# A three-layer graph network kernel: exact bf16 parts of the state transposed by DMA instead of TensorE, s spread through DRAM, and four groups under way in a written order of turns

## The chip, the cores and the metric

The kernel runs on one core of a Trainium2 chip. The metric is the device time in microseconds (us) of the program; lower is better. Below, PE is TensorE (PEld its weight loads), DVE is VectorE, ACT is ScalarE, POOL is GpSimd, and SP is SyncE, which issues the DMAs here.

## The reference, cut to what matters

There are 128 graphs of 128 nodes with 256 features each, in float32, and one 128x128 adjacency of zeros and ones per graph. Layer 0 normalizes x, runs three rounds of a gated graph network, and adds the result to x. Layer 1 normalizes again, runs one graph attention with scores from a single number per node, and adds its result.

```python
h = relu(layernorm(x))
for i in range(3):
    m = h @ weight[i]
    aggr = einsum('bst,bsd->btd', A, m)       # A = (adj != 0)
    gi = aggr @ w_ih.T + b_ih;  gh = h @ w_hh.T + b_hh
    r = sigmoid(i_r + h_r);  z = sigmoid(i_z + h_z)
    n = tanh(i_n + r * h_n)
    h = (1 - z) * n + z * h
x = x + h
h = relu(layernorm(x))
Wh = h @ W
s = Wh.sum(-1)
e = where(adj == 0, -inf, leaky_relu(s[:, :, None] + s[:, None, :], 0.2))
x = x + softmax(e) @ Wh
```

## The kernel before

**Tiling.** The graphs are worked on in 32 groups of four (`G = 4`, `NG = 32`). The state of a group lives in two forms: `rows`, with the nodes on the partitions, and `hT`, with the features on the partitions; both are 128 partitions x 1,024 float32. The weights are composed once at the start (`weights`): weight[i] and w_ih become one matrix for each round (`s_x0` to `s_x2`), beside `s_hh` for w_hh.

**A round (layer) of one group** has these steps:

- `node_sums` (L546 to L550) forms sums and differences of blocks of hT (tile `hs`, on POOL) and later of the edge sums (tile `gs`, on DVE).
- `edge_sums` (L498) multiplies by the adjacency. The adjacency is exact in bf16. The state is made so by splitting it into three bf16 parts: the upper halves of its float32 words, read in place with a stride (`top`), the upper halves of what is left (`r1`, POOL, L505), and what is left after that (`p3`, POOL, L508). Three bf16 matmuls then add up to the float32 result (L517, 24 matmuls a round), which ACT copies to `aT` (L521).
- `products` (L593) computes all gates with seven block products instead of eight (`hs` and `gs` are what this needs) in six PSUM banks `x_`, `y_` and `q_`, each for `rz` and `n`; ACT copies banks out (L613) and DVE adds (L616). Its matmuls stand on L576, or on L583 in the last layer, which produces rows.
- `gru` (L650) or, in the last layer, `gru_rows` (L687) applies the gates on ACT and DVE and writes the new hT, or x1.
- `T_to_rows` (L478) turns the new hT back into rows: eight TensorE transposes against an identity (L486) into two PSUM banks, and two ACT copies (L490). The first layer's hT comes from its rows in the same way in `rows_to_T` (L465, transposes on L472, copies on L475).

**The attention** (L764) computes s, one number per node (L772), spreads it across the partitions with four TensorE transposes per group (L781), adds and masks on DVE (L793 to L801), takes the exponential of the whole 128x512 tile on ACT (L803), masks and sums on DVE (L805, L807), transposes the result (L815), and multiplies (L532, L828).

**What sets the order.** Every step is entered in a list with its engine, a planned duration in ns and the buffers that it reads and writes (`op`). A planner (`Plan.run`) then simulates the engines and writes out one fixed order per engine. Gate products form a chain with due times: a turn of one group and one layer has 18,150 ns, and the turn number comes from `phase`. All other steps get a rank from the due times behind them, with a lead of `MARGIN`. Buffers of kind "all" rotate, those of kind "set" rotate by group, "free" ones are given to whoever comes first, and "turn" ones are given in the order of the turns. Three groups are under way (`SETS = 3`); a group's layers stand two turns apart:

```python
late = int(g == NG - 2 and layer > 0) - int(g == NG - 1)
return 3 * g + 2 * layer + late
```

So between two layers of a group there is one turn of another group. All DMAs are issued by SP, in order: x and the adjacency of a group (L737, L739), and the output (L836).

## Time and profile before

| | us |
|---|---|
| median of 3 runs | 2231.08 |
| runs | 2229.99 to 2231.71 |
| profiled execution | 2230.82 |
| its span | 2229.0 |

The mean granted clock of TensorE in the profiled execution is 0.995 of full speed. The costliest groups that bear on the change read as follows on the page (line, engine, operation, output<-input, shapes, count, then busy us, mean ns of one, and the idle time of that engine just before them with its releaser):

```profile
L546 POOL TENSOR_TENSOR hs<-hT 128x512 f32<-128x512 f32 x96 | 133.4, 1390 | 830.8 <-DVE hT L684 802.6
L505 POOL TENSOR_TENSOR r<-rows 128x512 f32<-128x512 f32 x192 | 209.8, 1106 | 38.2 <-ACT rows L490 27.2
L508 POOL TENSOR_TENSOR p<-r 128x512 bf16<-128x512 f32 x192 | 197.9, 1050 | 5.2
L517 PE MATMUL misc<-a,rows 128*128 128x128 bf16 x768 | 136.9, 219 | 0.1
L490 ACT COPY rows<-misc 128x512 f32<-128x512 f32 x128 | 74.4, 584 | 100.5 <-PE misc L486 96.9
```

The 830.8 us before L546 are idle time of POOL, which isn't needed then. A mean on PE is the time of one matmul from start to end, and neighbours overlap. The DMA issues of the page are (output<-input, queue, count, KB each, median us from issue to landing):

```profile
xt<-in_x_dram SPq DMA_DIRECT2D x32, 512.0 KB, 3.8
out_dram<-x SPq DMA_DIRECT2D x31, 512.0 KB, 3.0
at<-in_adj_dram SPq DMA_DIRECT2D x32, 256.0 KB, 2.9
```

### The profile page before, as it was taken

The page shows a single profiled execution, that of the slowest core. Times are in us where ns is not written, and L with a number is a line of the kernel's source. Part 1 is how long each engine was busy: PE and PEld are TensorE (multiplying, and loading weights), DVE is VectorE, ACT ScalarE, POOL GpSimd, SP SyncE. Part 2 cuts the span into 40 slices and gives each one's busy share as a digit, 9 for nine tenths or more (in the row PEclk, how much of TensorE's full clock was granted, in tenths as well). Part 3 has the DMA queues.
Part 4 walks back from the last instruction along what each step waited for, and adds up shares of the span by engine and source line. Part 5 has one row for each costly group of instructions (what it writes and reads, how often), then busy time and mean ns, then how long its engine had stood idle before and what let it go on. Part 6 is the DMA issues. An engine that isn't in the chain of part 4 may idle for free. (4 is left out here: it accounts for less than half of the span.)

```text
span 2229.0 us, 34912 instructions
## 1 busy us (share of the span) xinstructions
PE 2201.2 (99%) x13414; PEld 1967.8 (88%) x13414; DVE 1623.3 (73%) x3330; ACT 1295.0 (58%) x2396; POOL 909.0 (41%) x889
## 2 busy tenths in 40 slices
PE   8999999999999999999999999999999999999996
PEld 6889998889998889998899988899988899988895
DVE  5587777877677877677777778776778776778667
ACT  4565656655656655566656566556566555666454
POOL 5354444343434343434344443434343434344321
PEclk9999999999999999999999999999999999999998
DMA  3000000000000000000000000000000000000000
GB/s 105 10 15 20 25 17 23 15 24 20 24 15 25 15 20 25 25 15 24 15 20 25 20 19 15 25 20 24 15 24 15 20 24 24 15 20 10 11 11 19
DMA packets 55671, 47.59 MB, mean 21 GB/s; under 512 B 3280, under 2 KB 55248, under 8 KB 55504
## 3 DMA queue, kind: packets, MB, share of 16 engines
q1 hardware_dynamic: 55504, 45.36, 6.5%
q8 instruction: 105, 1.72, 0.3%
q14 instruction: 62, 0.51, 0.1%
HBM read 28.58 MB, written 16.78 MB: 20 GB/s over the span
## 5 line engine op out<-in xcount | busy, mean ns | idle before, releaser
L546 POOL TENSOR_TENSOR hs<-hT 128x512 f32<-128x512 f32 x96 | 133.4, 1390 | 830.8 <-DVE hT L684 802.6
L616 DVE TENSOR_TENSOR t_rz<-t_rz,q_rz 128x512 f32<-128x512 f32 x192 | 131.6, 685 | 268.2 <-ACT t_rz L613 229.0
L613 ACT COPY t_rz<-y_rz 128x512 f32<-128x512 f32 x192 | 111.8, 583 | 318.7 <-PE y_rz L576 224.0
L719 POOL TENSOR_TENSOR x<-xt,u 128x512 f32<-128x512 f32 x64 | 84.8, 1324 | 357.6 <-ACT u L715 357.6
L505 POOL TENSOR_TENSOR r<-rows 128x512 f32<-128x512 f32 x192 | 209.8, 1106 | 38.2 <-ACT rows L490 27.2
L508 POOL TENSOR_TENSOR p<-r 128x512 bf16<-128x512 f32 x192 | 197.9, 1050 | 5.2
L576 PE MATMUL y_rz<-hs,s_hh 128*128 128x256 f32 x768 | 199.0, 381 | 0.0
L576 PE MATMUL y_rz<-gs,s_x 128*128 128x256 f32 x768 | 197.2, 379 | 0.0
L576 PEld LDWEIGHTS y_rz<-gs,s_x 128*128 128x128 f32 x768 | 145.7, 190 | 19.7
L576 PEld LDWEIGHTS y_rz<-hs,s_hh 128*128 128x128 f32 x768 | 138.9, 190 | 15.4 <-ACT t_rz L613 0.3
L616 DVE TENSOR_TENSOR t_n<-t_n,q_n 128x512 f32<-128x512 f32 x192 | 131.2, 683 | 13.4 <-ACT t_n L613 7.9
L517 PE MATMUL misc<-a,rows 128*128 128x128 bf16 x768 | 136.9, 219 | 0.1
L517 PE MATMUL misc<-a,p 128*128 128x128 bf16 x768 | 136.9, 219 | 0.0
L517 PE MATMUL misc<-a,r 128*128 128x128 bf16 x768 | 136.9, 219 | 0.0
L613 ACT COPY t_n<-y_n 128x512 f32<-128x512 f32 x192 | 112.6, 586 | 40.6 <-PE y_n L576 21.8
L576 PE MATMUL x_rz<-hT,s_hh 128*128 128x256 f32 x512 | 132.5, 381 | 3.1 <-DVE hT L684 3.1
L490 ACT COPY rows<-misc 128x512 f32<-128x512 f32 x128 | 74.4, 584 | 100.5 <-PE misc L486 96.9
L576 PE MATMUL x_rz<-aT,s_x 128*128 128x256 f32 x512 | 131.7, 380 | 0.0
L521 ACT COPY aT<-misc 128x512 f32<-128x512 f32 x192 | 111.5, 581 | 17.7 <-PE misc L517 14.1
L828 PE MATMUL misc<-w,uT 128*128 128x256 f32 x512 | 117.0, 381 | 0.3 <-ACT uT L537 0.2
L576 PE MATMUL y_n<-gs,s_x 128*128 128x256 f32 x384 | 115.8, 383 | 0.0
L676 ACT ACTIVATE u<-u,bias_i 128x512 f32<-128x512 f32 x128 | 92.5, 724 | 38.8 <-DVE u L667 38.8
(218 smaller groups left out, 6157.2 us busy)
## 6 DMA issues: line engine op xcount, KB each, us to landing
xt<-in_x_dram SPq DMA_DIRECT2D x32, 512.0 KB, 3.8
out_dram<-x SPq DMA_DIRECT2D x31, 512.0 KB, 3.0
at<-in_adj_dram SPq DMA_DIRECT2D x32, 256.0 KB, 2.9
rz<-in_L_gnn_w_ih_dram SPq DMA_DIRECT2D x1, 768.0 KB, 5.2
h<-in_L_gnn_weight_dram SPq DMA_DIRECT2D x3, 256.0 KB, 5.4
rz<-in_L_gnn_w_hh_dram SPq DMA_DIRECT2D x1, 768.0 KB, 8.1
out_dram<-x SPq DMA_DIRECT2D x2, 256.0 KB, 2.1
e<-in_L_gnn_b_ih_dram SPq DMA_DIRECT2D x1, 256.0 KB, 5.3
```

The costliest lines, as they stand in the source:

```text
L490: op("ACT", 590, lambda n=n, ps=ps: nc.scalar.copy(ap(dst)[:, 2 * n:2 * n + 2, :], ap(ps)), [ps], [(dst, 2 * n, 2 * n + 2)])
L505: op("POOL", 1290, lambda part=part: nc.gpsimd.tensor_tensor(ap(r1)[:, part], ap(rows)[:, part], top(rows)[:, part], OP.subtract), [(rows, ...
L508: op("POOL", 1290, lambda part=part: nc.gpsimd.tensor_tensor(ap(p3)[:, part], ap(r1)[:, part], top(r1)[:, part], OP.subtract), [(r1, n, n ...
L517: nc.tensor.matmul(flat(ps)[:, b * N:(b + 1) * N], m[:, b, k * P:(k + 1) * P], ap(a)[:, b, :], start=(i == 0), stop=(i == 2))
L521: op("ACT", 590, lambda k=k, ps=ps: nc.scalar.copy(ap(dst)[:, k, :], flat(ps)), [ps], [(dst, 2 * k, 2 * k + 2)])
L546: op(eng, cost, lambda: sub(ap(w)[:, 0:2, :], blocks()[:, 1::2, :], blocks()[:, 0:2, :], OP.subtract), [t], [(w, 0, 2)])
L576: nc.tensor.matmul(ap(bank)[:, half, :], ap(w)[:, i - 1, q, :], source(t, sums), start=(first and c == 0 and m == 0), stop=False, skip_gro ...
L613: op("ACT", 590, lambda: nc.scalar.copy(ap(t), ap(y)), [y], [t])
L616: op("DVE", 690, lambda: nc.vector.tensor_tensor(ap(t), ap(t), ap(q), OP.add), [q], [t])
L676: op("ACT", 723, lambda j=j, cols=cols: nc.scalar.activation(ap(u)[:, cols], ap(u)[:, cols], AF.Tanh, bias=ap(W["bias_i"])[:, 2 * KD + j:2 ...
L719: op("POOL", 1290, lambda cols=cols, part=part: nc.gpsimd.tensor_tensor(part(x1), part(xt), ap(u)[:, cols], OP.add), [(xt, lo, hi), (u, lo ...
L828: nc.tensor.matmul(ap(ps)[:, b, :], ap(uT)[:, k, (m + b) * N:(m + b + 1) * N], ap(w1)[:, k, :], start=(k == 0), stop=(k == KD - 1))
```

## The change

- **Transposes.** `split` makes three bf16 parts of the state as tiles (`pl`): ACT copies to bf16, POOL subtracts, ACT copies the rest, POOL subtracts again, for each half. `turned_parts` transposes them with two DMA transposes of 128x1536 bf16 (`plT`), issued by SP. The edge matmuls of layers 1 and 2 read `plT`, those of layer 0 read `pl`. Where a float32 form is needed, POOL adds the three parts: `whole_T` for the first layer's hT, `whole_rows` for the rows of the last layer. The first three groups (`EARLY`) still get their first hT through TensorE.
- **Attention.** s goes to DRAM and comes back spread over the partitions by two DMAs, except in the last two groups, which keep the TensorE transposes. The exponential takes minus the row maximum as its bias and sums as it goes, in four pieces per group; a subtraction, a mask and a sum on DVE go, and four operations on 128x4 come. It stands behind a later turn than before.
- **Order.** Four groups are under way. The turns are written out: in the steady part layer 0 of group g, layer 1 of group g-1, layer 2 of group g-2. `rows`, `pl`, `plT`, `hs`, `aT`, `gs` are now two buffers each, given in order of the turns. The planner ranks steps through the waiting lines for those buffers too, and places the exponential as soon as its turn is reached. MARGIN is 5,000.
- **Buffers.** x is read a second time, into x1, instead of being kept; the normalization works in place. The weights' temporary homes at the start move to other tiles (not shown).

```diff
-SETS = 3
+SETS = 4
+EARLY = 3
 SLOT = 18150
-MARGIN = 4000
+MARGIN = 5000
...
+        after = [list(u) for u in users]
+        for tag, w in waiting.items():
+            n = self.tags[tag][0]
+            for b, nxt in zip(w[n:], w):
+                for i in b.users:
+                    after[i].append(nxt.users[0])
...
+        behind = [(i, self.marks[mark]) for i, mark in self.turns if mark in self.marks]
+        for i, j in behind:
+            nodes[i][5] = rank[j] + nodes[i][1]
+            users[j].append(i)
+            missing[i] += 1
+        rank_all()
+        for i, _ in behind:
+            rank[i] = -float("inf")
...
-        "xt": (3, "all", work, [P, G, D]), "at": (1, "all", work, [P, G, N]),
-        "a": (4, "all", work, [P, G, N]),
-        "r1": (2, "free", work, [P, G, D]), "p3": (2, "free", work, [P, G, D]),
-        "hT": (1, "set", work, [P, KD, GN]), "rows": (1, "set", work, [P, G, D]),
-        "hs": (1, "set", work, [P, 4, H]), "aT": (1, "set", work, [P, KD, GN]),
-        "gs": (1, "set", work, [P, 4, H]),
+        "at": (1, "all", work, [P, G, N]), "a": (6, "all", work, [P, G, N]),
+        "hT": (1, "set", work, [P, KD, GN]), "rows": (2, "turn", work, [P, G, D]),
+        "pl": (2, "turn", work, [P, 2, 3, GN]), "plT": (2, "turn", work, [P, 2, 3, GN]),
+        "hs": (2, "turn", work, [P, 4, H]), "aT": (2, "turn", work, [P, KD, GN]),
+        "gs": (2, "turn", work, [P, 4, H]),
...
-        "u": (2, "free", work, [P, G * D]), "d": (2, "free", work, [P, GN]),
+        "u": (2, "free", work, [P, G * D]), "d": (4, "free", work, [P, GN]),
...
+        "s_all": (1, "all", work, [P, G, N]), "s_out": (2, "all", dram, [G, N]),
...
+    def split(src):
+        pl = buf("pl")
         for n in range(2):
...
+            r = buf("d")
+            def half(n=n):
+                return ap(src).rearrange("p a b -> p (a b)")[:, n * GN:(n + 1) * GN]
+            op("ACT", 590, lambda n=n, half=half: nc.scalar.copy(ap(pl)[:, n, 0], half()),
+               [(src, 2 * n, 2 * n + 2)], [(pl, n, n + 1)])
+            op("POOL", 1110, lambda n=n, half=half, r=r: nc.gpsimd.tensor_tensor(
+                ap(r), half(), ap(pl)[:, n, 0], OP.subtract),
+               [(src, 2 * n, 2 * n + 2), (pl, n, n + 1)], [r])
+            op("ACT", 590, lambda n=n, r=r: nc.scalar.copy(ap(pl)[:, n, 1], ap(r)),
+               [r], [(pl, n, n + 1)])
+            op("POOL", 1060, lambda n=n, r=r: nc.gpsimd.tensor_tensor(
+                ap(pl)[:, n, 2], ap(r), ap(pl)[:, n, 1], OP.subtract), [r], [(pl, n, n + 1)])
+        return pl
+    def turned_parts(pl):
+        plT = buf("plT")
         for n in range(2):
+            op("SP", 2000, lambda n=n: nc.sync.dma_start_transpose(
+                ap(plT)[:, n].rearrange("p c (m q) -> p (c m) q", q=P),
+                ap(pl)[:, n].rearrange("p c m -> p (c m)")), [(pl, n, n + 1)], [(plT, n, n + 1)])
+        return plT
+    def whole(plT, dst, view, part, units):
+        for n in range(2):
+            op("POOL", 1110, lambda n=n: nc.gpsimd.tensor_tensor(
+                view(ap(dst), n), part(ap(plT)[:, n, 2]), part(ap(plT)[:, n, 1]), OP.add),
+               [(plT, n, n + 1)], units(dst, n))
+            op("POOL", 1110, lambda n=n: nc.gpsimd.tensor_tensor(
+                view(ap(dst), n), view(ap(dst), n), part(ap(plT)[:, n, 0]), OP.add),
+               [(plT, n, n + 1)], units(dst, n))
+    def whole_T(plT, hT):
+        whole(plT, hT,
+              lambda t, n: t.rearrange("p k (n b m) -> p n b k m", n=2, m=N)[:, n],
+              lambda t: t.rearrange("p (b k m) -> p b k m", b=2, k=KD),
+              lambda t, n: [(t, n, n + 1), (t, 2 + n, 3 + n)])
+    def whole_rows(plT, rows):
+        whole(plT, rows,
+              lambda t, n: t[:, :, n * P:(n + 1) * P],
+              lambda t: t.rearrange("p (g m) -> p g m", g=G),
+              lambda t, n: [t])
...
+    def edge_sums(parts, a, dst, rows):
         for k in range(KD):
             ps = buf("misc")
             def edges(k=k, ps=ps):
                 for b in range(G):
-                    for i, m in enumerate((top(rows), top(r1), ap(p3))):
+                    n, at = (b // 2, (b % 2) * D + k * P) if rows else (k, b * P)
+                    for i in range(3):
                         nc.tensor.matmul(flat(ps)[:, b * N:(b + 1) * N],
-                                         m[:, b, k * P:(k + 1) * P], ap(a)[:, b, :],
+                                         ap(parts)[:, n, i, at:at + P], ap(a)[:, b, :],
-            op("PE", 700, edges, [rows, r1, p3, a], [ps], [dst])
+            op("PE", 700, edges, [parts if rows else (parts, k, k + 1), a], [ps], [dst])
...
             op("POOL", 1290, lambda cols=cols, part=part: nc.gpsimd.tensor_tensor(
-                part(x1), part(xt), ap(u)[:, cols], OP.add),
-               [(xt, lo, hi), (u, lo, hi)], [(x1, lo, hi)])
+                part(x1), part(x1), ap(u)[:, cols], OP.add),
+               [(u, lo, hi)], [(x1, lo, hi)])
...
+    turns = [(0, 0), (1, 0), (2, 0), (0, 1), (1, 1), (3, 0), (0, 2), (2, 1), (1, 2)]
+    for g in range(4, NG - 3):
+        turns += [(g, 0), (g - 1, 1), (g - 2, 2)]
+    turns += [(NG + i, layer) for i, layer in (
+        (-3, 0), (-2, 0), (-4, 1), (-5, 2), (-1, 0), (-3, 1), (-4, 2), (-2, 1), (-1, 1), (-3, 2),
+        (-2, 2), (-1, 2))]
+    assert sorted(turns) == [(g, layer) for g in range(NG) for layer in range(L)]
...
-        op("SP", 1500, lambda: nc.sync.dma_start(ap(xt), x[graphs].rearrange("b n d -> n b d")),
+        plan.phase = phase(g, 0)
+        plan.due = (plan.phase - 1) * SLOT
+        rows0, at, a, hT = buf("rows"), buf("at"), buf("a"), buf("hT")
+        op("SP", 1500, lambda: nc.sync.dma_start(ap(rows0), x[graphs].rearrange("b n d -> n b d")),
+           [], [rows0])
...
-        plan.due = (3 * g + 6) * SLOT
-        rows, hT = buf("rows"), buf("hT")
-        normed(xt, rows)
-        rows_to_T(rows, hT)
+        plan.due = (phase(g, L - 1) + 2) * SLOT
+        normed(rows0, rows0)
         for layer in range(L):
+            plan.phase = phase(g, layer)
+            pl = split(hT if layer else rows0)
+            if layer or g >= EARLY:
+                plT = turned_parts(pl)
+                if not layer:
+                    whole_T(plT, hT)
+            else:
+                rows_to_T(rows0, hT)
             hs, aT, gs = buf("hs"), buf("aT"), buf("gs")
-            node_sums(hT, hs, "POOL", 1290, 780)
-            edge_sums(rows, a, aT)
+            node_sums(hT, hs, "POOL", 1390, 940)
+            edge_sums(plT if layer else pl, a, aT, not layer)
             node_sums(aT, gs, "DVE", 690, 422)
-            plan.phase = phase(g, layer)
+            if layer == L - 1:
+                rows, x1, h1 = buf("rows"), buf("x1"), buf("h1")
+                whole_rows(plT, rows)
+                op("SP", 1500, lambda: nc.sync.dma_start(
+                    ap(x1), x[graphs].rearrange("b n d -> n b d")), [], [x1])
             plan.cursor = plan.phase * SLOT
             if layer < L - 1:
                 gru(layer, hT, hs, aT, gs)
-                rows = buf("rows")
-                T_to_rows(hT, rows)
-        plan.due = (3 * g + 7) * SLOT
-        x1, h1 = buf("x1"), buf("h1")
-        gru_rows(L - 1, hT, hs, aT, gs, rows, xt, x1)
+        plan.due = (phase(g, L - 1) + 3) * SLOT
+        gru_rows(L - 1, hT, hs, aT, gs, rows, x1)
...
-        def spread():
-            for b in range(lo, hi):
-                nc.tensor.transpose(flat(p_s)[:, b * N:(b + 1) * N],
-                                    ap(s)[:, b:b + 1].to_broadcast([P, P]), ident)
-        op("PE", 110 * n, spread, [s], [p_s], [e])
-        op("DVE", cost, lambda: nc.vector.tensor_tensor(
-            es().rearrange("p b n -> p (b n)"), es().rearrange("p b n -> p (b n)"),
-            flat(p_s)[:, lo * N:hi * N], OP.add), [p_s], [e])
+        if g < NG - 2:
+            s_out, s_all = buf("s_out"), buf("s_all")
+            op("SP", 500, lambda: nc.sync.dma_start(
+                ap(s_out)[part].rearrange("g n -> n g"), small(s)), [s], [s_out])
+            op("SP", 500, lambda: nc.sync.dma_start(
+                ap(s_all)[:, part],
+                ap(s_out)[part].rearrange("(o g) n -> o g n", o=1).to_broadcast([P, n, N])),
+               [s_out], [s_all])
+            spread = lambda: ap(s_all)[:, part]
+        else:
+            s_all = buf("misc")
+            spread = lambda: flat(s_all)[:, lo * N:hi * N].rearrange("p (b n) -> p b n", n=N)
+            def turn_s():
+                for b in range(lo, hi):
+                    nc.tensor.transpose(flat(s_all)[:, b * N:(b + 1) * N],
+                                        ap(s)[:, b:b + 1].to_broadcast([P, P]), ident)
+            op("PE", 110 * n, turn_s, [s], [s_all], [e])
+        op("DVE", cost, lambda: nc.vector.tensor_tensor(es(), es(), spread(), OP.add), [s_all], [e])
...
-        op("DVE", cost, lambda: nc.vector.tensor_tensor(es(), es(), wide(top), OP.subtract),
-           [top], [e])
-        op("ACT", 3200, lambda: nc.scalar.activation(es(), es(), AF.Exp), [], [e],
-           turn=(g + 2, 0, "n"))
-        op("DVE", cost, lambda: nc.vector.tensor_tensor(es(), es(), ap(a)[:, part], OP.mult),
-           [(a, lo, hi)], [e])
-        op("DVE", cost, lambda: nc.vector.tensor_reduce(ap(den)[:, part], es(), AX.X, OP.add),
-           [e], [den])
-        op("DVE", 170, lambda: nc.vector.reciprocal(ap(rden)[:, part], ap(den)[:, part]),
-           [den], [rden])
+        op("DVE", 150, lambda: nc.vector.tensor_scalar(small(low), small(top), -1.0, None,
+                                                       op0=OP.mult), [top], [low])
+        def exps():
+            for b in range(lo, hi):
+                nc.scalar.activation(ap(e)[:, b, :], ap(e)[:, b, :], AF.Exp, bias=ap(low)[:, b:b + 1],
+                                     accum_out=ap(den)[:, b:b + 1])
+        op("ACT", 2600 + 300 * n, exps, [low], [e, den], turn=(g + 2, 1, "rz"))
+        op("DVE", 150, lambda: nc.vector.tensor_scalar(
+            small(some), small(top), -BIG / 1e3, None, op0=OP.is_gt), [top], [some])
+        op("DVE", 150, lambda: nc.vector.tensor_tensor(small(den), small(den), small(some), OP.mult),
+           [some], [den])
+        op("DVE", 170, lambda: nc.vector.reciprocal(small(rden), small(den)), [den], [rden])
+        op("DVE", 150, lambda: nc.vector.tensor_tensor(small(rden), small(rden), small(some), OP.mult),
+           [some], [rden])
```

## The prediction

> **What bounds the kernel now.** I read the page's busy shares first, then the stretches of the span engine by engine, then the waits of TensorE, and last the groups and the order in time of what the change takes out.
>
> The busy shares (engine, busy us, share of the span, instructions):
>
> ```profile
> PE 2201.2 (99%) x13414; PEld 1967.8 (88%) x13414; DVE 1623.3 (73%) x3330; ACT 1295.0 (58%) x2396; POOL 909.0 (41%) x889
> ```
>
> A busy TensorE (PE) may hide waits, so the next view cuts the span into its beginning, its middle and its end (stretch, its length, busy us of each engine, granted clock, DMA share, GB/s):
>
> ```profile
> 0.00:20.00 20.00, 15.88 (x98) 12.45 (x98) 11.64 (x27) 10.38 (x21) 8.36 (x14) 1.00 0.89 230
> 40.00:60.00 20.00, 16.68 (x95) 11.63 (x94) 10.33 (x17) 7.97 (x15) 12.12 (x12) 0.83 0.00 1
> 80.00:2160.00 2080.00, 2079.89 (x12756) 1867.67 (x12755) 1532.53 (x3138) 1227.11 (x2269) 855.30 (x829) 1.00 0.06 20
> 2180.00:2200.00 20.00, 16.24 (x102) 14.69 (x101) 16.02 (x42) 10.80 (x18) 2.57 (x3) 0.98 0.00 1
> 2200.00:2229.00 29.00, 16.92 (x69) 12.55 (x68) 17.17 (x49) 8.27 (x16) 3.96 (x5) 0.78 0.10 36
> ```
>
> For 2,080 us PE idles 0.1 us, at full clock; all of its 27.8 us of idle time lie in the first 80 us (10.4) and the last 69 us (17.3). The waits of PE say the same (who waited for whom, us in total, times, longest):
>
> ```profile
> PE misc L815 <- DVE e L805: 6.6, 2, 3.5
> PE x_rz L576 <- DVE hT L684: 3.1, 1, 3.1
> PE q_rz L576 <- DVE gs L546: 2.9, 2, 2.2
> ```
>
> Two times, one time, two times: none of them belongs to the repeated part. So the middle is one queue of TensorE work with no gap, and an instruction taken out of it is worth its place in that queue. That place isn't its mean duration, because neighbours overlap. The order in time shows it (start us, us, instruction, count):
>
> ```profile
> 1031.32 0.60 PE L486 MATMUL misc<-ident,hT 128*128 128x128 f32 x4
> 1031.76 1.03 PE L576 MATMUL y_rz<-hs,s_hh 128*128 128x256 f32 x4
> 1032.62 1.03 PE L576 MATMUL y_rz<-gs,s_x 128*128 128x256 f32 x4
> ```
>
> Four transposes hold the queue from 1031.32 to 1031.76: 0.44 us, 110 ns each. Their group has 275 ns as the mean of one; using that would overrate the change 2.5 times. (Gate products: four in 0.86 us, 216 ns each.)
>
> **What the Trainium skill says.** "TensorE: Matmul & The Clock Gate", Part 4 (PE-mode transpose), gives about 275 ns for one transpose in a kernel's context; the trace's mean is the same 275 ns, but only 110 ns of it is exclusive. "DMA: Bandwidth & Descriptors", Latency and other measured facts, has DMA transposes moving 261 GB/s in one kernel. "VectorE: DVE Perf Modes", The three transpose paths, has 1,309 ns for one 128x128 bf16 block through the DMA crossbar. No DMA transpose is in the trace of before, so the last two are the ends between which I must choose. "ScalarE: Activation LUTs", What ACT_TABLE_LOAD costs, prices an activation with a pointer bias at 280 ns + 0.833 ns per element; for 512 elements that is 707 ns, and the trace has 724 ns (tanh, L676).
>
> **The change part by part.**
>
> *Taken out of PE's queue.* T_to_rows goes (L486, 512 transposes). Of the 256 of rows_to_T (L472), the 24 of groups 0 to 2 stay: 232 go. Of the 128 that spread s (L781), those of the last two groups stay (8): 120 go. The built order confirms 864 fewer transposes, and all other TensorE work is there in equal number: 2,304 edge matmuls (only their stationary operand comes from other tiles), all gate products, the attention. 864 x 0.110 us = 95.0 us. PE's work falls from 2,201 to 2,106 us, from 68.8 to 65.8 us per group.
>
> *Added to the DMA queue of SP.* 192 - 6 = 186 transposes of 128x1536 bf16 (384 KB), two for each turn, six for each group. Bounds for one: nearest rows, a plain load of 512 KB lands in 3.8 us and one of 256 KB in 2.9 us, so some 3.3 us for 384 KB even at the rate of a plain load; upper end, twelve blocks at 1.309 us in a row, 15.7 us. At 261 GB/s the bytes take 1.5 us, and the plain loads show about 2 us of fixed latency. I take 4 us. Six are 24 us; with two x loads (7.6), adj (2.9), the output (3.0) and the trip of s through DRAM (two small DMAs, some 5 us together from the 2.1 us of the 256 KB output) SP has about 42 us of DMA latency per 65.8 us, even if none overlapped.
>
> *What hides their latency.* The turns now run four groups apart: layer l of a group is followed by three turns of other groups before its layer l+1; before, by one. In the built order of PE the edge matmuls that read a transposed part stand at the start of the turn before the one that needs them. From the end of a turn to its final hT takes about 7 us in the trace, the split (ACT, POOL, ACT, POOL, twice) some 10 us on shared engines, two transposes at 4 us another 8: 25 us. Up to those edge matmuls there are two turns, 2 x 21.9 = 44 us. Some 19 us remain spare.
>
> *Waits added, and who stands behind.* SP runs in order: a transpose waits for POOL's third part and for the buffer plT, and behind it stand x, adj, the output and s; two more reads of x now wait for an output to land. On POOL the sums that rebuild rows and hT (L542, L545) wait for the transposes, and behind them stand the node sums hs, which the gates' second product reads. These lie inside the same 19 us.
>
> *POOL.* Out: 209.8 + 197.9 (L505, L508). In: split, 192 x 1.106 + 192 x 1.050 = 414; rebuilding, (58+58+64+64) x 1.106 = 270, taking the rate of L505 for bf16 inputs in a strided view, which no row shows. 909 - 408 + 414 + 270 = 1,185 us, 55%.
>
> *ACT.* Out: 128 x 0.584 (L490) and 58 x 0.589 (L475), 109. In: 384 bf16 copies x 0.584 = 224; the exponential in four pieces, 128 x 0.387 by the formula above less the 20 it had, and reading the accumulators, 40 more. 1,295 - 109 + 224 + 40 = 1,450 us, 68%.
>
> *DVE.* Out: L801, L805, L807, 22.8 + 36.3 + 21.3 = 80. In: four 128x4 operations per group at 0.17, 22; the first addition now reads two SBUF operands beside a busier POOL, up to 31 x (1.308 - 0.680) = 19. About 1,580 us, 74%.
>
> None of the three becomes the bound by its sum. Their pauses are shorter, though, and DVE operations with two SBUF inputs are slower while POOL works: 0.68 us for L717 in the quiet end of the trace against a mean of 1.17.
>
> *Beginning and end.* In before the second turn slot is empty: at 46.1 us PE waits for hT of the only group under way, and works at 0.83 of the clock in that stretch. After, groups 0, 1 and 2 fill it: -6 us at most. Against that, the bf16 parts of group 0 need ACT and POOL four times before its first edge matmuls: +3 us. At the end three last layers follow one another, which crowds DVE; the instructions after the last gate product are the same list: 0 to +5. Together I take 0, with -8 and +8 as ends.
>
> *The sum.* 2,229.0 - 95.0 + 0 + 4 (a few new waits; before has under 1 us in the middle, and the slack above is worked out from means) = 2,138 us of span. The profiled execution took 2,230.8, 1.8 more than its span, and lies 0.3 below the median, so the forecast is 2,140 us.
>
> **The rivals.** *A: the forecast holds,* 2,125 to 2,155: PE still without gaps in the middle. For it: 0.1 us of idle in 2,080, 864 transposes less, about 19 us of slack per turn.
>
> *B: part of it comes back as waits on elementwise engines.* A gs or hs that is late costs PE 1.4 to 2.2 us each time (L546, above). Once per group, 32 x 1.5 = 48 us: 2,140 + 48 = 2,188. For it: ACT and POOL gain 155 and 276 us of work while the span shrinks, 95 us of filler that covered PSUM copies is gone. Against: 90 of the 96 turns still have filler between the two y products, where before had 91.
>
> *C: the transposes become the bound, and the kernel is slower.* One mechanism: SP's queue must pass six of them per group. If a block costs 1.309 us and blocks don't overlap, 186 x 15.7 = 2,920 us, and with the 18 us before the first edge matmul and the 35 us after the last gate product that are in the trace of before, about 2,975. It decides from 68.8 / 6 = 11.5 us for each if the other DMAs overlap, from (68.8 - 18.5) / 6 = 8.4 us if they don't; at 11.5 they would just eat the gain. For it: no row shows the operation, all go through one queue. Against: it needs twelve independent blocks to move without any overlap, at 25 GB/s, where the plain loads of the trace reach 230 in the first stretch.
>
> *D: the change doesn't do what it says.* Excluded for its main part by the built order: the transposes are gone from PE.
>
> **How the numbers follow.** A 0.58, B 0.22, C 0.18, something between that lands on the old time 0.02. Time: that of A, 2,140. The range takes A whole and B up to twice its wait less a part, 2,124 to 2,210, which leaves out C and little else. Differences under 0.2% (4.5 us) are no change by what this kernel's measurement can tell: faster 0.80, same 0.02, slower 0.18.
>
> **What would show it.** Right: PE's busy time near 2,106 us and under 1 us of idle per 100 in the middle; the rows of L486 gone; a DMA transpose landing within 3 to 6 us; POOL near 55%, ACT near 68%. B would show as PE waits on DVE gs, POOL hs or ACT aT with counts near 32 or 96. C would show as PE edge matmuls, and POOL's sums, waiting for plT, with SP's DMA queue filled end to end. I would be wrong, too, if the ends of the span grow by over 10 us.

## The result: 16.6 percent slower, and the profile after

The changed kernel takes 2600.5 us in the median of four runs (2599.6 to 2605.6), the kernel before 2230.5 beside it: a ratio of 1.166, with a 95% interval of 1.164 to 1.168. The profiled span is 2598.2 us.

The busy shares of the changed kernel:

```profile
PE 2233.4 (86%) x12550; PEld 1956.6 (75%) x12550; DVE 1906.7 (73%) x3363; ACT 1424.1 (55%) x2815; POOL 1275.3 (49%) x1133
```

PE has the predicted 864 instructions less and yet is busy for 32 us longer than before. The prediction's sum for its work, at the pace of the kernel before, is 2,106 us; 127 us of longer busy time, with the mean granted clock at 0.93, and 365 us of idle time stand beside that (2,106 + 127 + 365 = 2,598). The cut into stretches (stretch, its length, busy us of PE, PEld, DVE, ACT and POOL, granted clock, DMA share, GB/s) shows that the loss is in the repeated part:

```profile
80.00:2480.00 2400.00, 2075.10 (x11676) 1823.11 (x11675) 1774.95 (x3073) 1320.63 (x2603) 1200.41 (x1058) 0.93 0.25 55
```

Before, PE idled 0.1 us in 2,080 there; now 325 in 2,400. Who waited for whom in the changed kernel (us in total, times, longest):

```profile
DVE e L879 <- DMA s_all<-s_out: 344.4, 30, 14.2
POOL rows L542 <- DMA plT<-pl: 325.1, 28, 13.6
ACT rz L754 <- DVE t_rz L672: 309.2, 29, 13.8
...
PE q_rz L639 <- DVE t_rz L672: 218.6, 29, 10.4
```

Counts of 28 to 30 mean once per group. One such chain in order of time (start us, us, instruction, idle time before it and its releaser):

```profile
1019.71 0.37 SPq L863 DMA_DIRECT2D s_out<-s  x1
...
1029.92 0.34 SPq L865 DMA_DIRECT2D s_all<-s_out  x1
1030.37 4.54 SPq L534 DMA_TRANSPOSE plT<-pl  x2
1034.02 0.69 DVE L879 TENSOR_TENSOR e<-e,s_all 128x512 f32<-128x512 f32 x1 [11.26 <-DMA s_all<-s_out]
...
1036.08 0.68 DVE L672 TENSOR_TENSOR t_rz<-t_rz,q_rz 128x512 f32<-128x512 f32 x1
...
1036.79 1.15 POOL L542 TENSOR_TENSOR rows<-plT 128x512 f32<-128x512 bf16 x1 [12.74 <-DMA plT<-pl]
...
1036.91 2.05 PE L639 MATMUL q_rz<-s_hh,hs 128*128 128x256 f32 x4 [7.21 <-DVE t_rz L672]
```

The store of s starts at 1019.71; the load that spreads it can't start before it has landed, at 1029.92. DVE stands still for 11.26 us at the addition that needs s (L879). Behind that addition in DVE's fixed order stand the gate additions t_rz and t_n (L672), and on them waits PE, for 7.21 us. After that wait four gate products take 2.05 us, where the trace of before has 1.03. On SP the transposes are queued behind the load of s_all, and POOL's rebuilding of rows waits for them, 12.74 us.

The DMA issues of the changed kernel (KB each, median us from issue to landing):

```profile
s_all<-s_out SPq DMA_DIRECT2D x30, 256.0 KB, 4.9
plT<-pl SPq DMA_TRANSPOSE x186, 4.0
...
s_out<-s SPq DMA_DIRECT2D x30, 2.0 KB, 9.1
```

The transposes cost what was taken, 4.0 us. The trip of s takes 9.1 + 4.9 = 14.0 us instead of 5, most of it in the store of 2 KB. What doesn't show in a profile is what the planner counted: for each of the two transfers 500 ns and a fixed 2,500 ns from a transfer to the step that uses it (`LAG`), together 6 us.

### The profile page after: what moved, and what is told of

The parts are those of the page before. It is cut to its first block, busy times and chain, and to the rows that moved or that the text cites. A ratio compares the mean times of both kernels' runs of the same rounds, so it can differ in the third digit from the quotient of the medians.

```text
span 2598.2 us, 34734 instructions
## 1 busy us (share of the span) xinstructions
PE 2233.4 (86%) x12550; PEld 1956.6 (75%) x12550; DVE 1906.7 (73%) x3363; ACT 1424.1 (55%) x2815; POOL 1275.3 (49%) x1133
## 4 chain that ended last, share of the span: by engine, by line
DVE 34%; PE 30%; DMA 18%; issue 9%; ACT 9%; POOL 1%; DVEq 0%; ACTq 0%; POOLq 0%
DMA s_out<-s 11%; PE y_rz L632 6%; DMA s_all<-s_out 5%; DVE d L735 4%; PE x_rz L632 4%; DVE d L738 3%; PE q_rz L639 3%; PE q_rz L632 3%; DVE u L720 3%; DVE hw L842 3%; PE y_n L632 3%; DVE x L780 3%; PE misc L573 2%; DVE gs L602 2%; DVE st L474 2%
## 5 line engine op out<-in xcount | busy, mean ns | idle before, releaser
L521 POOL TENSOR_TENSOR d<-hT,pl 128x512 f32<-128x512 f32 x128 | 157.7, 1234 | 323.9 <-ACT pl L519 296.7
L526 POOL TENSOR_TENSOR pl<-d,pl 128x512 bf16<-128x512 f32 x192 | 248.2, 1295 | 100.7 <-ACT pl L524 100.6
L639 PE MATMUL q_rz<-s_hh,hs 128*128 128x256 f32 x256 | 98.1, 520 | 228.6 <-DVE t_rz L672 218.6
L879 DVE TENSOR_TENSOR e<-e,s_all 128x512 f32<-128x512 f32 x30 | 21.8, 727 | 344.4 <-DMA s_all<-s_out 344.4
L542 POOL TENSOR_TENSOR rows<-plT 128x512 f32<-128x512 bf16 x64 | 80.9, 1264 | 325.1 <-DMA plT<-pl 325.1
L672 DVE TENSOR_TENSOR t_rz<-t_rz,q_rz 128x512 f32<-128x512 f32 x192 | 130.5, 680 | 60.1 <-ACT t_rz L669 29.3
L519 ACT CAST pl<-hT 128x512 bf16<-128x512 f32 x128 | 78.7, 620 | 145.2 <-DVE hT L740 145.2
L573 PEld LDWEIGHTS <-plT 128*128 128x128 bf16 x1536 | 121.2, 116 | 28.1 <-issue 16.1
L735 DVE TENSOR_TENSOR d<-hT,u 128x512 f32<-128x512 f32 x128 | 133.0, 1039 | 6.8 <-ACT u L732 5.5
L672 DVE TENSOR_TENSOR t_n<-t_n,q_n 128x512 f32<-128x512 f32 x192 | 130.4, 679 | 9.1 <-PE q_n L632 5.1
L573 PE MATMUL misc<-a,plT 128*128 128x128 bf16 x1536 | 128.7, 251 | 8.1 <-DVE x L922 8.1
L524 ACT CAST pl<-d 128x512 bf16<-128x512 f32 x192 | 118.5, 618 | 27.5 <-POOL d L521 27.4
L775 POOL TENSOR_TENSOR x<-x,u 128x512 f32<-128x512 f32 x64 | 89.4, 1399 | 88.8 <-ACT u L771 48.0
```

Of the source, the lines that this page charges most:

```text
L521: op("POOL", 1110, lambda n=n, half=half, r=r: nc.gpsimd.tensor_tensor(ap(r), half(), ap(pl)[:, n, 0], OP.subtract), [(src, 2 * n, 2 * n + ...
L524: op("ACT", 590, lambda n=n, r=r: nc.scalar.copy(ap(pl)[:, n, 1], ap(r)), [r], [(pl, n, n + 1)])
L526: op("POOL", 1060, lambda n=n, r=r: nc.gpsimd.tensor_tensor(ap(pl)[:, n, 2], ap(r), ap(pl)[:, n, 1], OP.subtract), [r], [(pl, n, n + 1)])
L542: op("POOL", 1110, lambda n=n: nc.gpsimd.tensor_tensor(view(ap(dst), n), part(ap(plT)[:, n, 2]), part(ap(plT)[:, n, 1]), OP.add), [(plT, n ...
L573: nc.tensor.matmul(flat(ps)[:, b * N:(b + 1) * N], ap(parts)[:, n, i, at:at + P], ap(a)[:, b, :], start=(i == 0), stop=(i == 2))
L639: nc.tensor.matmul(ap(bank)[:, m, half * P:(half + len(chunk)) * P], source(t, sums)[:, m * N:(m + 1) * N], ap(w)[:, i - 1, q:q + len(chun ...
```

## The experiments

The first theory was the chain just shown: the trip of s through DRAM and what stands behind DVE's wait for it. Its rivals were SP's queue, with the transposed parts (`plT`) that come late, and elementwise work (the additions, products and copies on DVE, ACT and POOL). Later runs ask whether the instructions are slow or the order was planned for durations that the chip doesn't keep. All ratios are against the kernel before, run beside each.

**s on TensorE again**, everything else of the change kept:

```diff
-        if g < NG - 2:
+        if g < 0:
```

> The changed kernel with one part undone: s is spread by four TensorE transposes in all 32 groups, not only in the last two; everything else stays. Theory 1 (the late s holds DVE, whose fixed order has the gate additions behind it, so PE waits and its clock falls): nearly the whole loss goes; PE work is 2,106 + 30 x 0.44 = 2,119 us, with 28 us of idle time at the ends and a few waits about 2,150 us, mean clock back over 0.98, POOL's 325 us of waiting for plT gone with it. Theory 2 (the loss is in the DMA transposes, the order of turns or POOL's added work, and s only coincides with it): it stays above 2,450 us, with PE waiting for transposed parts or for sums of POOL.

2339.1 us, ratio 1.049 (1.047 to 1.050). Taking the trip away gives back 261 us; yet the run takes 190 us more than the first theory allowed. There is a second cause.

**The true cost of the trip given to the planner**, instructions unchanged:

```diff
-            op("SP", 500, lambda: nc.sync.dma_start(
+            op("SP", 7500, lambda: nc.sync.dma_start(
                 ap(s_out)[part].rearrange("g n -> n g"), small(s)), [s], [s_out])
-            op("SP", 500, lambda: nc.sync.dma_start(
+            op("SP", 2500, lambda: nc.sync.dma_start(
                 ap(s_all)[:, part],
...
```

> The changed kernel with s still going through DRAM; only the planned costs of the two small DMAs are changed, from 500 to 7,500 and 2,500 ns, so that with the planner's lag of 2,500 they stand at 10.0 and 5.0 us, near the 9.1 and 4.9 us that the trace shows. The planner then writes the DVE addition of s later in DVE's order. Theory 1: the DMAs are as slow as before but nothing stands behind them, so about 2,140 to 2,180 us. Theory 3 (it is SP's queue, held by the wait of the second DMA for the first, that makes the transposes late): the queue is held as long as before, so it stays above 2,400 us, and PE or POOL waits for plT.

2354.0 us, ratio 1.056 (1.054 to 1.058): 246 us come back although each store still takes over 8 us, but the 2,140 to 2,180 us of the first theory aren't reached. Two waits of this run (SPq is SP's DMA queue):

```profile
DVE e L879 <- DMA s_all<-s_out: 114.0, 28, 5.8
...
SPq L865 <- DMA s_out<-s: 243.3, 29, 10.6
```

DVE's wait for s fell from 344 to 114 us, while SP's queue is held for the store nearly as long as in the changed kernel (243 against 273 us). So SP's queue as the main loss is excluded, and most of what the trip cost lay in the order that was planned around it. The edit moves other steps as well as L879; how much is due to L879 alone isn't shown.

**The store written as it lies**, 128 runs of 16 bytes rather than 512 single elements. The numbers are then read back in the wrong order, so this kernel's attention scores are not the reference's:

```diff
-                ap(s_out)[part].rearrange("g n -> n g"), small(s)), [s], [s_out])
+                ap(s_out)[:, part], small(s)), [s], [s_out])
...
-                ap(s_out)[part].rearrange("(o g) n -> o g n", o=1).to_broadcast([P, n, N])),
+                ap(s_out).rearrange("n g -> (n g)").rearrange("(o g n) -> o g n", o=1, g=G).to_broadcast([P, n, N])),
```

> The changed kernel, but s is stored as it lies, four neighbouring numbers per partition (128 runs of 16 bytes, not 512 single numbers of 4 bytes), and read back as one run of 512 numbers: the numbers of s meet the wrong columns of e, so the softmax is over wrong scores; all sizes and waits are the same. If the single 4-byte elements make the store slow, it lands in 2 to 4 us and not in 9.1, DVE waits about 5 us in a group and the time falls to some 2,250 to 2,350 us. If it is the write to DRAM and its receipt or the queue, it lands in 8 to 9 us and the time stays near 2,600 us.

2343.5 us in one run. DMA issues of this run:

```profile
s_all<-s_out SPq DMA_DIRECT2D x30, 256.0 KB, 4.0
...
s_out<-s SPq DMA_DIRECT2D x30, 2.0 KB, 1.4
```

So 512 separate elements make the store long, not DRAM: the same 2 KB land in 1.4 us as 128 runs. With the trip this short, though still planned as before, 257 us come back, nearly as many as without it. The Trainium skill, "DMA: Bandwidth & Descriptors", Why small descriptors are slow (HBM only), names an overhead per packet and 32 bytes of metadata per DMA operation that are fixed, however few bytes move; the traces agree in direction (9.1 against 1.4 us), and don't show which of these makes the difference.

**Only the trip of s, put into the kernel before:**

```diff
-        op("PE", 110 * n, spread, [s], [p_s], [e])
...
+            op("SP", 500, lambda: nc.sync.dma_start(
+                ap(s_out)[part].rearrange("g n -> n g"), ap(s)[:, part]), [s], [s_out])
+            op("SP", 500, lambda: nc.sync.dma_start(
+                ap(s_all)[:, part],
...
```

> The kernel before with one part of the change alone: s through DRAM with the same two DMAs and the same planned costs, PE transposes and the order of turns as before. Theory 1: the wait of DVE comes with it, some 11 us in each of 30 groups, of which a part is covered: 2,400 to 2,600 us. Theory 2: about 2,220 to 2,235 us, since 120 PE transposes go and DVE had room.

2288.4 us in one run: 58 us slower than before, between the 2,400 and more that the first theory expected and the 2,220 to 2,235 of the second. Its waits:

```profile
DVE e L807 <- DMA s_all<-s_out: 113.6, 30, 7.8
...
PE misc L827 <- DVE e L817: 49.0, 29, 3.5
```

The same wait of DVE is there (its addition is L807 in this kernel), but in that order it mostly delays the attention's own transposes (L827): PE is idle for 86 us in all, where the kernel before has 28. What a late s costs depends on what was planned behind it.

**All turns on TensorE**, so that only the four-group order, the splitting and the attention's edits remain (T_to_rows and rows_to_T as before, plT and its sums gone, three buffers of rows; edit not shown):

> The changed kernel with s turned on TensorE and with all turns of the state on TensorE again: what is left of the change is the order of four groups, the splitting and the attention's edits. If TensorE's sum bounds it, as the prediction said, the 864 turns put 95 us back on its 2,106 us and the run takes 2,220 to 2,260 us, and POOL loses the 210 us of rebuilding; the kernel with s alone on TensorE (2,339) would then be slower in spite of 95 us less work, and its loss would lie in the turned parts and what waits for them. If the second loss lies in the order itself (the late second read of x, the slower VectorE operations), this run keeps it and takes over 2,330 us.

2309.6 us, ratio 1.036 (1.034 to 1.038). A loss of 80 us remains without one DMA transpose and without the trip. It lies between the two forecasts, so neither the transposed parts nor the four-group order alone explains the second loss. In this trace and that of s on TensorE, a wait for the second read of x is prominent (the latter's waits):

```profile
POOL x L775 <- DMA x<-in_x_dram: 120.7, 25, 13.0
```

That made the two buffers of x1 a suspect. **Three of them**, with s on TensorE:

```diff
-        "x1": (2, "all", work, [P, G, D])
+        "x1": (3, "all", work, [P, G, D])
```

> The kernel with s turned on TensorE, with three buffers of x1 in place of two, so that the second read of x need not wait for the output to leave the same buffer. If the late second read is the second cause, the stall of 3.7 us in each cycle goes and with it the clock's fall: 2,339 falls by some 120 to 190 us, to 2,150 to 2,220. If it is only the wait that ends last beside VectorE operations that run longer than the planner counts, another wait takes its place and the time stays within 50 us, 2,290 to 2,340.

2362.2 us, 23 more than with two and far from the 2,150 to 2,220 that it would take as the cause. The wait for the read left the list of long waits and others came (waits of PE in this run):

```profile
PE y_n L632 <- ACT t_n L669: 50.9, 23, 2.3
PE y_rz L632 <- ACT t_rz L669: 45.7, 62, 3.6
```

The most visible wait wasn't the cause. **The planner's costs** for VectorE and GpSimd were the other suspect. One gate operation, d<-hT,u, is planned with 690 ns in both kernels; that fits the kernel before (first line) and no longer the changed one (second line):

```profile
L679 DVE TENSOR_TENSOR d<-hT,u 128x512 f32<-128x512 f32 x128 | 87.5, 685 | 3.8 <-ACT u L676 3.8
L735 DVE TENSOR_TENSOR d<-hT,u 128x512 f32<-128x512 f32 x128 | 133.0, 1039 | 6.8 <-ACT u L732 5.5 <-POOL pl L526 1.1
```

23 lines of numbers were set to the means of the profile of s on TensorE; no instruction was changed:

```diff
-            op("POOL", 1060, lambda n=n, r=r: nc.gpsimd.tensor_tensor(
+            op("POOL", 1280, lambda n=n, r=r: nc.gpsimd.tensor_tensor(
...
-            op("DVE", 690, lambda j=j, d=d, cols=cols: nc.vector.tensor_tensor(
+            op("DVE", 1055, lambda j=j, d=d, cols=cols: nc.vector.tensor_tensor(
                 ap(hT)[:, j, :], ap(u)[:, cols], ap(d), OP.add), [(u, lo, hi), d], [(hT, lo, hi)])
...
-            node_sums(aT, gs, "DVE", 690, 422)
+            node_sums(aT, gs, "DVE", 830, 815)
```

> The kernel with s turned on TensorE, and the planner's costs of VectorE and GpSimd operations set to what the profile of that kernel measured (for instance 1,055 in place of 690 ns for the last addition of the gate, 1,280 in place of 1,060 for the split); instructions are the same, only their order changes. If the second loss is an order planned with times that the chip does not keep, it falls to 2,150 to 2,230 with the waits on transfers smaller. If the two buffers of x1 are the cause whatever the order, it stays within 40 us of 2,339.

2207.1 us, ratio 0.990 (0.988 to 0.991): 132 us gained by numbers alone, and 1% faster than before. POOL's wait for the second read of x is longer here (208.9 us) than in the slower kernel (120.7), another sign that it wasn't the cause. With three buffers of x1 as well:

> Both of the two edits before: three buffers of x1 and measured costs. If both causes are real and separate, this is the fastest, 2,130 to 2,190 us, and beats the kernel before. If only one is real, it equals that one's run within 20 us. Should VectorE, at 1,866 us busy, bound it with its chains, it stays above 2,250.

2197.2 us, ratio 0.985 (0.984 to 0.987); 10 us for the buffer here, where it cost 23 before. That misses the 2,130 to 2,190 forecast for two separate causes and lies within 20 us of the costs alone: only the costs are shown as a cause, and VectorE isn't the bound. **The costs taken a second time** from that kernel's profile:

> The fastest kernel so far (2,197 us), with the costs taken once more, from its own profile. If the order is now bound by TensorE's 2,138 us and the 30 us at both ends, it stays within 10 us of 2,197. If its costs still mislead the planner, it gains 10 to 30 us.

2188.7 us: 8.5 us less, inside the spread of such orders (below).

**The whole change, unchanged in every instruction, with all these costs true** (7,500 and 2,500 ns for the trip, and the 23 lines measured with s on TensorE):

> The whole change, s through DRAM and all state turns by DMA, with every cost the planner uses set to a measured one: the two small transfers (7,500 and 2,500 ns of SP) and the VectorE and GpSimd operations as in the run with s on TensorE (2,207 us). If the loss of the change was only that its order was planned with times the chip does not keep, this falls from 2,354 to 2,190 to 2,220 and beats the kernel before. If the trip through DRAM costs by itself (a store of 9 us in SP's queue, with the transposes behind it), it stays 30 us or more above 2,207.

2171.8 us, ratio 0.974 (0.972 to 0.975): the fastest of all runs, below the 2,190 to 2,220 expected, 58 us faster than before and 429 faster than the change as it was. Its busy shares and repeated part:

```profile
PE 2123.7 (98%) x12550; PEld 1884.9 (87%) x12550; DVE 1857.8 (86%) x3363; ACT 1432.3 (66%) x2815; POOL 1298.5 (60%) x1133
...
80.00:2080.00 2000.00, 1977.07 (x11745) 1761.77 (x11744) 1736.94 (x3094) 1333.20 (x2612) 1227.76 (x1062) 1.00 0.31 67
```

PE idles 23 us in 2,000 and the clock is 1.00 there. The trip of s is as long as it was, but none of its 30 additions on DVE waits for it (first line, no idle time before it; then one of them in order of time, SP's and DVE's instructions):

```profile
L879 DVE TENSOR_TENSOR e<-e,s_all 128x512 f32<-128x512 f32 x30 | 21.9, 730 | 0.0
...
1060.86 0.52 SPq L863 DMA_DIRECT2D s_out<-s  x1
...
1069.97 0.34 SPq L865 DMA_DIRECT2D s_all<-s_out  x1
...
1075.12 0.68 DVE L879 TENSOR_TENSOR e<-e,s_all 128x512 f32<-128x512 f32 x1
```

L879 starts 14.3 us after the store was issued, as in the changed kernel (1019.71 to 1034.02), but without idle time before it: DVE's other work is planned into the gap.

**The two wrong costs apart.** The true elementwise costs with the trip still planned at 500 ns:

> The changed kernel with the measured VectorE and GpSimd costs, but with the two transfers of s still at 500 ns each. If the two wrong costs act separately, this keeps most of what the s trip cost (some 100 to 250 us above 2,172: 2,270 to 2,420), with VectorE waiting for s_all 30 times. If the VectorE and GpSimd costs alone were the cause and the wait for s only their consequence, it falls to 2,170 to 2,200.

2385.4 us, ratio 1.069 (1.068 to 1.071); DVE waits for s_all again:

```profile
DVE e L879 <- DMA s_all<-s_out: 247.8, 30, 12.4
```

Planned costs, in us, with the times together:

| | elementwise as written | elementwise measured |
|---|---|---|
| trip of s at 500 ns | 2600.5 | 2385.4 |
| trip of s as measured | 2354.0 | 2171.8 |

Either error costs 180 to 250 us, whether the other is there or not: they act separately. With **VectorE's costs alone** corrected, and the trip's:

> The changed kernel with the true cost of s and the measured costs of VectorE alone; GpSimd's stay as they were (1,060 to 1,110 ns where 1,260 to 1,350 were measured). If VectorE's underestimate is the cause, this comes within 20 us of 2,172. If GpSimd's is, it stays near the 2,354 that the true cost of s alone gave.

2189.1 us: VectorE's underestimate makes nearly all of the second part. GpSimd's is worth 17 us here, no more than the spread of orders; it wasn't corrected alone.

**Luck of the order?** The same costs shifted by 4 percent up and down:

> The fastest kernel (2,172 us) with its measured VectorE and GpSimd costs shifted by 4 percent up or down, alternately. If that time comes from costs near enough to what the chip takes, this order takes 2,160 to 2,200 as well. If it was a lucky order among many, this lands at 2,220 or more.

2194.8 us, inside the expected range: costs that are nearly right give 2,170 to 2,200. Some 25 to 30 us of the 2,172 may be luck, not the 429. The kernel of 2,600 us isn't one unlucky order either: of the runs that transpose the state by DMA, the four with VectorE's and GpSimd's costs as written, and the trip away, short or planned at its length, take 2,339 to 2,362 us; the eight with VectorE's costs corrected, and the trip away or planned at its length, take 2,172 to 2,207 (two of them follow). **A third buffer of x1** in the fastest kernel gave no gain but 2201.2 us, 29 more, and so belongs to the same spread:

> The fastest kernel (2,172 us) with three buffers of x1. It took 10 us off where s was turned on TensorE. If TensorE's sum of 2,106 us and the two ends bound it now, it gains 0 to 10 us, 2,160 to 2,172; a gain of 20 us or more would mean that the second read of x still held it.

**All turns on TensorE, with costs from its own profile:**

> The kernel with all turns on TensorE (2,310 us) with the costs of VectorE and GpSimd set to those measured in its own profile. If TensorE's sum bounds a well-planned kernel of this kind, it comes to 2,230 to 2,250, the time of the kernel before, and the DMA transposes are worth the difference to 2,207, less than half of the 84 us that the 768 turns come to at 110 ns. If the four-group order is worse in itself, it stays above 2,270.

2244.4 us, ratio 1.006 (1.005 to 1.008). So the four-group order is as good as the old one to within 14 us, once it is planned with true costs, and moving all 864 transposes off TensorE is worth 2244.4 - 2171.8 = 72.6 us between these two orders. Each is one order out of a spread of 25 to 30 us: against the run with shifted costs the same 864 are worth 50 us. The old order had no such loss to recover: PE idled 0.1 us in its repeated part.

**Less GpSimd work**: the first layer's hT made on TensorE in every group (in the kernel of 2,197 us):

```diff
-EARLY = 3
+EARLY = 32
```

> The fastest kernel so far (2,197 us), with the first layer's transposed state of every group made on TensorE from the float32 rows (232 transposes back, 25.5 us at 110 ns, and 58 copies for ACT) and no longer rebuilt by GpSimd (116 operations less, some 150 us of GpSimd time); the DMA transposes stay. If a busy GpSimd is what makes VectorE's operations long, VectorE's busy time falls by 30 us or more from 1,887 us, with its instructions unchanged. The time then rises by at most 25 us if TensorE is the bound, and by less, or falls, if VectorE's chains still hold the kernel.

2194.6 us against 2197.2, no different: the 25.5 us that the 232 transposes cost by the prediction's count don't show beside the spread. Its busy shares:

```profile
PE 2154.8 (98%) x12902; PEld 1917.1 (87%) x12902; DVE 1773.0 (81%) x3363; ACT 1447.7 (66%) x2873; POOL 1151.3 (53%) x1017
```

VectorE's instructions are the same in number and kind, and take 114 us less than the 1,887.2 of the run it is compared with, while GpSimd is busy for 171 us less.

## Why the prediction was wrong, by its own steps

- **"864 x 0.110 us = 95.0 us", PE's work "falls from 2,201 to 2,106 us": right** in what it counts. Between two kernels planned with measured costs 72.6 us of it are seen, in one order of each. Against the kernel before, in spans, 2,229.0 - 2,170.2 = 58.8 us: PE is busy for 17.7 us over 2,106 (2,123.7), and idles 18.7 more than before (46.5 against 27.8); 95 - 17.7 - 18.7 = 58.6.
- **"I take 4 us" for a DMA transpose: right,** 4.0. With it rival C fell: the kernel of 2,172 us passes all 186 through SP while PE idles 23 us in 2,000.
- **The trip of s, "some 5 us together": wrong,** 14.0 us. It was priced from a large store with long runs; here each run is one element. The planner's 6 us were as short, so comparing the prediction with the plan gave no warning; only the trace of the store itself shows its length.
- **"Waits added, and who stands behind": the step that failed first.** It went through SP's queue and POOL's sums and left out DVE's wait at L879. Behind that stand t_rz and t_n, and behind these PE; DVE waits there for 344 us in all. Taking the trip away gives back 261 us, planning it at its true length 246.
- **"About 1,580 us, 74%. None of the three becomes the bound by its sum": wrong in DVE's size,** though none became the bound. DVE takes 1,907 us, 1,866 with s on TensorE. The note that DVE is slower beside a busy POOL was in the text, but it was priced for one operation of the attention only (19 us), where POOL's new work runs beside the gates: d<-hT,u takes 1,039 ns where it took 685. The four 128x4 operations, 22 us in the sum, take 67 (6.2 + 9.9 + 28.7 + 22.2). ACT (1,424 against 1,450 forecast) and POOL (1,275 against 1,185) were nearer.
- **"Some 19 us remain spare", "+4 (a few new waits)": wrong by two orders of magnitude** (365 us of idle time and 127 of longer busy time), and for a reason that covers both errors; this is the step that failed most. The slack was worked out from what operations take on the chip. But the order was fixed beforehand from the planner's numbers: 500 ns and the fixed 2,500 for each transfer of s, 690 ns for gate operations that take 910 to 1,040 here. Slack in the kernel doesn't help where the plan doesn't know that it is needed. The prediction has no term for the plan's costs. With them corrected and every instruction kept, 429 of the 2,601 us go. The last layer of the kernel before had shown the trouble: the prediction quotes 1.17 us for L717, which the planner counts as 690 ns.
- **Rival B** named the kind of wait (PE behind elementwise engines) and gave it 1.5 us per group. It was 7.5 (218.6 / 29) for one of these waits alone, and the mean clock was 0.93 instead of 0.995.

What isn't settled is which of the 23 corrected VectorE and GpSimd lines carry the second 182 us; only the split into two engines was tried (18 lines of VectorE, 5 of GpSimd).

## What to carry to other kernels

Where an order is fixed from planned costs, a new operation's cost in the plan is part of the change: compare each planned duration with the trace before judging the operation itself. For each wait that is added, write down what stands next on the waiting engine. The longest wait on a list is only a suspect; here removing its cause without correcting the plan made the kernel slower.

## What the runs showed of the hardware

VectorE's additions and products with both inputs in SBUF slow down while GpSimd works; those with one input in PSUM don't. All four lines are the same operation and shape. The first, from the kernel before, and the second, from the changed kernel, have t_n in SBUF; the last two, also from the changed kernel, have a PSUM bank instead (y_n, x_n). The second number after the count is the mean in ns:

```profile
L664 DVE SCALAR_TENSOR_TENSOR u<-t_n,bias_h,rz 128x256 f32<-128x256 f32 x128 | 61.9, 483 | 11.6 <-ACT rz L661 7.8
L720 DVE SCALAR_TENSOR_TENSOR u<-t_n,bias_h,rz 128x256 f32<-128x256 f32 x128 | 98.5, 770 | 24.3 <-ACT rz L717 20.1
...
L720 DVE SCALAR_TENSOR_TENSOR u<-y_n,bias_h,rz 128x256 f32<-128x256 f32 x64 | 30.6, 479 | 28.4 <-ACT rz L726 21.7 <-ACT rz L717 5.6 <-PE y_n L632 1.1
L720 DVE SCALAR_TENSOR_TENSOR u<-x_n,bias_h,rz 128x256 f32<-128x256 f32 x64 | 30.3, 474 | 2.9 <-ACT rz L726 1.8 <-ACT rz L717 1.0
```

Sorted by what POOL did in the meantime, in the trace of the changed kernel: of d<-d,rz (L738), 79 that met no POOL work take 0.69 us, 36 that lie (nine tenths or more) beside it 1.47; t_rz<-t_rz,q_rz (L672), with q_rz in PSUM, takes 0.68 in both cases. Two inputs aren't the only condition: the conversion a<-at (L804), with one input in SBUF, takes 0.42 us in the two cases without POOL and 1.20 in the 28 beside it. The Trainium skill, "GPSIMD Engine Reference", 8. Key points, says that the two share SBUF interfaces, with contention for VectorE instructions in a 2-port performance mode or with two SBUF inputs; the traces agree for two inputs (whether L804 runs in such a mode no run shows), and put the price at a factor of about two for L738, less or more for others (1.9 for u<-t_n,bias_h,rz, 2.5 for x<-x,d on L780). Here the plan took VectorE's quiet durations, and they stopped being true when work was moved to GpSimd.
